# Eight smaller output-weight products in tiles 7 to 14 of the first head, a third query buffer, and last-head loads one a tile

## The chip, the cores and the metric

The kernel runs on one core of a Trainium2 chip. A core has five engines that run side by side and wait for each other by semaphores: TensorE (PE in the profile) multiplies, VectorE (DVE), ScalarE (ACT) and GpSimd (POOL) work on elements, and SyncE (SP) here only starts transfers. TensorE writes to PSUM, the others read PSUM (GpSimd does not) and SBUF. 16 DMA engines carry all transfers. The metric is the device time of one execution in microseconds (us); lower is better.

## The reference, cut to what matters

The input `x` has 2048 rows of 256. Two residual blocks follow, each normalised on the way in and on the way out:

- Attention, 16 heads of 128. The weights are 4-bit codes with a scale for every 32 input rows. `w = codes * scale`; q, k, v are `ln(x) @ w + b`; `attn = softmax(q k^T / sqrt(128))`; the heads' outputs are multiplied by the output weights `wo` (2048 by 256), and `bo` is added. `x = x + ln(that)`.
- A mixture of eight experts with top-2 routing, `silu(g) * u` between products of width 176, all experts computed and combined with the routing weights. `x = x + ln(that)`.

## The kernel before

**Tiles.** A step `g` of the main loop is one tile: 128 query rows `t` (0 to 15) of one head `h` (0 to 15), so 256 tiles and two steps to run empty. In each step TensorE makes the scores of 128 rows by 2048 keys in two halves (`scores_half`, L511, L512, L515: q and k are held as a high and a low 16-bit part, three products each). VectorE takes the row maximum of each half from PSUM (L516). ScalarE makes `p = exp(s - m)` with the row sums (`softmax`, L527). One step later ScalarE writes the normalised high part `ph` (L541), and VectorE the remainder `pl` in two halves (`low_half`, L556: p times the reciprocal sum, minus ph). SP transposes ph and pl by DMA (L544, L562) into `pth` and `ptl`. TensorE multiplies those with v, six matmuls to a piece, two pieces a step, 13 pieces behind the scores (`pv_part`, L582); every four tiles the result is evicted and written to DRAM (`ot_d`, L597 to L602).

**Work between.** `fill` gives each step one projection: q or k of the coming tiles and head (`proj_qk`) or v (`proj_v`). In the first six tiles of the first head two blocks of 128 rows of v are projected per step; ScalarE makes the high part and VectorE the low one (L269, L270), and the PSUM tile is free only then. Later projections go through `t32`, filled by ScalarE (L246, L277), from which GpSimd makes both parts (L247, L248, L278, L279). `weight_steps` loads and multiplies the q, k, v weights of the next pair of heads on GpSimd (L132, L138, L182, L184).

**Output weights.** They are loaded at the start, four pairs of codes and scales (`wo_raw`, L314 to L324), and multiplied on GpSimd by `dequant_wo` (L637 to L642), one pair in each of tiles 0 to 3 of the first head (L876).

**Buffers.** Most working tiles share one ring of 21 buffers of 4 KB a partition (`tag="x"`, `NX`): ph, pl, k, v, wo and its raw tiles, raw expert weights, reloaded attention outputs (`oi`), rows of x and others. A tile takes a buffer that has become free; if none is, the engine that writes it waits for the last reader of the one it takes. q has its own two buffers (L217); the last head puts two of its q tiles into the ring (`slot="x"`).

**Order.** Each engine runs its instructions in the order in which this program issues them. SP's order holds the transposes and, between them, the loads of the last heads: `early` (head 14, L793) loads `bo` and the first `oi`, `late` (head 15, L810) follows the tables `GW_LOAD` and `GW_SPLIT` (gate weights, loaded and split into two parts), `OI_LOAD` and `OI_USE` (attention outputs reloaded and multiplied by wo, `op_mm`, L712).

**Drain.** After the loop (L1107 on) the last pieces of v are multiplied, with output products `op_mm`, layer norms, transposes and the router between them; then the experts.

Of the kernel before, what the change touches and what calls it, by code (L numbers as in the profile page):

```python
# [8 lines left out]
F32 = mybir.dt.float32  # L9
F32R = mybir.dt.float32r  # L10
BF = mybir.dt.bfloat16
HP = mybir.dt.float16
# [3 lines left out]
ALU = mybir.AluOpType  # L16
# [5 lines left out]
D = 256  # L22
# [11 lines left out]
NX = 21  # L34
# [3 lines left out]
def sandwich(  # L38
# [22 lines left out]
    nc = tc.nc  # L61
# [45 lines left out]
    small = ctx.enter_context(tc.tile_pool(name="small", bufs=4))  # L107
# [85 lines left out]
    kqv = ctx.enter_context(tc.tile_pool(name="kqv", bufs=2))  # L193
# [20 lines left out]

    def kq_tile(which, h, b):
        if which == "q":
            return kqv.tile([128, 2, 512], HP, name="qT", bufs=2)  # L217
        if b % 2 == 0:
            KP[h] = kqv.tile([128, 2, 2, 512], HP, name="kT", tag="x", bufs=NX)
        return KP[h][:, b % 2]  # L220

    def proj_qk(which, h, b, tag="pj", wide=None, slot=None):
        w = W[(h // 2, which)]
        bias = bqs[:, IX[which], h : h + 1]
        ps = proj_psum(tag)
        col = bass.ts(h % 2, 128)
        n = 0
        for kc in range(2):
            for hl in range(2):
                nc.tensor.matmul(  # L230
                    ps, w[:, kc, col], xnT[:, 4 * b : 4 * b + 4, hl * 2 + kc, :],
                    start=(n == 0), stop=(n == 3),
                )
                n += 1
        if slot is None:
            t = kq_tile(which, h, b)
        else:
            t = kqv.tile([128, 2, 512], HP, name="qT_l", tag="x", bufs=NX)
        if wide is None:
            nc.scalar.activation(t[:, 0, :], ps, AF.Identity, bias=bias)  # L240
            pending.append(lambda: nc.vector.scalar_tensor_tensor(
                t[:, 1, :], ps, bias, t[:, 0, :], ALU.add, ALU.subtract
            ))
        else:
            t32 = wide.tile([128, 512], F32, name="t32")
            nc.scalar.activation(t32, ps, AF.Identity, bias=bias)  # L246
            nc.gpsimd.tensor_copy(t[:, 0, :], t32)  # L247
            nc.gpsimd.tensor_tensor(t[:, 1, :], t32, t[:, 0, :], ALU.subtract)  # L248
        (Q if which == "q" else K)[(h, b)] = t
# [31 lines left out]
    wo = []  # L281
    wo_raw = {}
# [3 lines left out]
    with tc.tile_pool(name="start", bufs=4) as st:  # L286
# [18 lines left out]
        for i, (which, codes, scales) in enumerate(  # L305
# [3 lines left out]
            cd = st.tile([128, 2, 256], F32, name="cd0", bufs=3)  # L309
# [4 lines left out]
        for q in range(4):  # L314
            hs = slice(4 * q, 4 * q + 4)
# [72 lines left out]
        mvs, rs, nbs, xns, xps = {}, {}, {}, {}, {}  # L388
# [111 lines left out]
    soft = soft_ctx.enter_context(tc.tile_pool(name="soft", bufs=2, reuse_waits="tile"))  # L500
# [73 lines left out]
    def pv_part(h, b, e):  # L574
# [11 lines left out]
        if e == 7:  # L586
# [20 lines left out]
    QK = {0: ("q", 0, 1), 2: ("k", 1, 0), 4: ("q", 0, 2), 6: ("k", 1, 1),  # L607
          8: ("q", 0, 3), 10: ("k", 1, 2), 12: ("q", 1, 0), 14: ("k", 1, 3)}

    def fill(h, t):  # L610
        p = h // 2
        if h == 0 and t < 6:
            proj_v(0, 4 + 2 * t, 2, "pv")
        if h == NH - 1:
            if t < 3:
                proj_qk("q", h, t + 1, wide=soft, slot="x" if t > 0 else None)
        elif t in QK:
            kind, dh, b = QK[t]
            if h + dh < NH:
                proj_qk(kind, h + dh, b, wide=soft)  # L620
        elif h % 2 == 0:
            if t in (3, 5) and h > 0:
                proj_v(p, 12 + (t - 3) // 2, 1, wide=soft)
            elif t == 7 and h > 0:
                proj_v(p, 14, 2, wide=soft)
            elif t >= 9 and p + 1 < NH // 2:
                proj_v(p + 1, (t - 9) // 2, 1, wide=soft)
        elif p + 1 < NH // 2:
            proj_v(p + 1, 4 + t // 2, 1, wide=soft)
# [4 lines left out]
            pv_part(n // 4, n % 4, e)  # L634


    def dequant_wo(q):  # L637
        sc, cd = wo_raw.pop(q)
        if q % 2 == 0:
            wo.append(kqv.tile([128, 8, D], BF, name="wo", tag="x", bufs=NX))  # L640
        hs = slice(4 * (q % 2), 4 * (q % 2) + 4)
        nc.gpsimd.tensor_tensor(wo[q // 2][:, hs], cd, sc, ALU.mult)  # L642

    def bias_row():
        pb = psA.tile([128, 512], F32, name="pb", tag="pj")
# [21 lines left out]
    def load_gu(src, i, pool, tag, bufs, eng=None):  # L667
        kc, eh = divmod(i, 2)
        stg = pool.tile([128, 4, I], F32, name="gu_raw", tag=tag, bufs=bufs)
        (eng or nc.sync).dma_start(  # L670
            out=stg,
            in_=src.rearrange("e (kc p) i -> kc p e i", p=128)[kc][:, 4 * eh : 4 * eh + 4],
        )
        return stg
# [25 lines left out]
    gw, crow, brow = None, None, None  # L700
    gst = {}
# [75 lines left out]
    def ln_c(b):  # L777
# [1 line left out]

    X1 = {}  # L780
    XV = x.rearrange("b (c p t) d -> p (b c) t d", p=128, t=4)
    GW_LOAD = {0: 1, 3: 2, 5: 3}
    GW_SPLIT = {4: 0, 6: 1, 8: 2, 10: 3}
    OI_LOAD = {
        2: (0, 1, 0), 4: (0, 1, 1), 6: (0, 1, 2), 9: (1, 0, 0), 10: (1, 0, 1),
        12: (0, 0, 3), 13: (0, 1, 3), 14: (1, 0, 2),
    }
    OI_USE = {
        4: (0, (0,)), 5: (0, (1,)), 6: (0, (2,)), 8: (1, (0,)), 9: (1, (1,)), 10: (1, (2,)),
        14: (0, (3,)), 15: (1, (3,)),  # L790
    }

    def early(t):  # L793
        nonlocal crow, brow
        if t == 7:
            cb = kqv.tile([128, 2, D], F32, name="crow", tag="x", bufs=NX)
            crow, brow = cb[:, 0], cb[:, 1]
            nc.sync.dma_start(out=brow, in_=bo.partition_broadcast(128))
        if t == 9:
            gst["b3"] = bias_row()  # L800
        if t == 11:
            bias_row2(gst.pop("b3"))
        if t == 13:
            nc.gpsimd.tensor_tensor(crow, crow, brow, ALU.add)
        if t in (8, 10, 12):
            load_oi(0, 0, t // 2 - 4)
        if t == 14:
            gst[0] = load_gu(wg, 0, kqv, "x", NX)

    def late(t):  # L810
        nonlocal gw
        if t == 3:
            proj_ctx.close()
            rp = ctx.enter_context(tc.tile_pool(name="gw", bufs=1, side="right"))
            gw = rp.tile([128, 2, 2, NCH, 128], F32R)
        if t in OI_USE:
            op_mm(0, *OI_USE[t], "pj", 2)
        if t in GW_SPLIT:
            split_gu(gw, GW_SPLIT[t], gst.pop(GW_SPLIT[t]), True)
        if t in GW_LOAD:  # L820
            i = GW_LOAD[t]
            gst[i] = load_gu(wg, i, kqv, "x", NX)
        if t in OI_LOAD:
            load_oi(*OI_LOAD[t])
        if t == 8:
            X1[0] = kqv.tile([128, 4, D], F32, name="x1_0", tag="x", bufs=NX)
            nc.sync.dma_start(out=X1[0], in_=XV[:, 0])

# [3 lines left out]
    for g in range(NS + 2):  # L832
        h, t = divmod(g, NT)
        live = g < NS
        if live:
            m = small.tile([128, 8], F32, name="m", bufs=6)
            s0 = scores_half(h, t, 0, m)
            if g == 0:
                proj_v(0, 0, 2)
                proj_v(0, 2, 2, "pv")  # L840
        if prev is not None:
            recip(prev[2])
        if prev2 is not None:
            low_half(1, *prev2)
        flush()
        if defer:
            pv_unit(2 * g - 1)
            defer = False
        pv_unit(2 * g)
        if prev is not None:  # L850
            prev = (*prev, high_part(*prev))
        if live:
            s1 = scores_half(h, t, 1, m)
            negmax(m)
            p = softmax((s0, s1), m)
        if prev is not None:
            low_half(0, *prev)
        prev2 = prev
        first = live and (2 * g + 1 - PVLAG) % 8 == 0
        if not first:  # L860
            pv_unit(2 * g + 1)
        if live:
            fill(h, t)
        if first and h == NH - 1:
            defer = True
        elif first:
            pv_unit(2 * g + 1)
        if live:
            prev = (h, t, m, p)
        else:  # L870
            prev = None
        if live:
            weight_steps(h, t)
        if h == 0 and t in (8, 9):
            tail_consts(t - 8)
        if g < 4:  # L876
            dequant_wo(g)
        if h == NH - 2:
            early(t)
        if h == NH - 1:  # L880
            late(t)
        if g == NS:
            ln_a(0)
        if g == NS + 1:
            load_oi(1, 0, 3)
            ust = [load_gu(wu, 0, kqv, "x", NX)]
            ust += [load_gu(wu, i, kqv, "x", NX) for i in range(1, 4)]
            ln_b1(0)
# [222 lines left out]
    uw = uwp.tile([128, 2, 2, NCH, 128], F32R)  # L1111
    d0 = load_d(0)
    d1 = load_d(4)
    op_mm(1, 0, (0, 1), "s")
    ln_b2(0)
    split_gu(uw, 0, ust[0], True)
    ln_c(0)
# [2 lines left out]
    tr(0, 0, "s")  # L1120
    tr(0, 1, "s")
    split_gu(uw, 1, ust[1], False)
    op_mm(1, 0, (2, 3), "s")
    for j in range(4):
        load_oi(1, 1, j)
    router_a(0, "s")
# [50 lines left out]
    for q in range(4 * NCH + 2):  # L1177
        b, c = divmod(q, NCH)
# [60 lines left out]
```

## Time and profile before

| what | us |
|---|---|
| median of three runs | 1842.27 (1839.41 to 1844.51) |
| profiled execution, and its span | 1839.29, 1837.5 |
| TensorE busy | 1780.7 (97%) |
| VectorE busy | 1635.1 (89%) |
| ScalarE busy | 1371.9 (75%) |
| GpSimd busy | 943.3 (51%) |
| L642, the four products for wo | 9.4 (2.36 each), from 41.6 to 60.7 us |
| L556, pl, 512 instructions | 730.3 (1.426 each; 1.265 at least, 4.340 at most) |

A line of a group names the source line, the engine, the operation and `output<-inputs`, with the count, busy time and mean. A line in order of time begins with start and duration; in brackets stands the idle time before it and what ended it. In busy time by stretch each engine has its busy us and instructions, then the granted TensorE clock (1.00 is full), the mean busy share of the DMA engines and their rate. A wait is `who <- for whom: us in all, times, longest`. SPq is SP's queue of transfers.

### The profile page before, as it was taken

What the parts mean: (1) busy time and instruction counts of PE and PEld (TensorE: products, weight loads), DVE (VectorE), ACT (ScalarE), POOL (GpSimd) and SP (SyncE); (2) the same over time, 40 slices, a digit from 0 to 9 for tenths busy, and PEclk for the clock granted to TensorE, in tenths of its full rate; (3) what the DMA queues carried; (4) which work ended last, traced back from release to release, by engine and by line L of the source; (5) the groups of instructions that cost most, each with busy time, mean ns of one, the idle gap of its engine ahead of it and who ended that gap; (6) DMA issues with size and microseconds to landing.
All of it is one profiled execution on the core that took longest, in us unless ns stands there. A gap on an engine that the chain in (4) does not pass through costs nothing. (4 is left out here: it accounts for less than half of the span.)

```text
span 1837.5 us, 25510 instructions
## 1 busy us (share of the span) xinstructions
PE 1780.7 (97%) x8890; PEld 936.4 (51%) x8890; DVE 1635.1 (89%) x2269; ACT 1371.9 (75%) x1732; POOL 943.3 (51%) x911
## 2 busy tenths in 40 slices
PE   7699999999999999999999999999999999899997
PEld 4344444444444444444444444444444444588886
DVE  7899999999999999999999999999999978558665
ACT  5688888888888888888888888888888877322232
POOL 3456556565656565656565656566444332323232
PEclk9899999999999999999999999999999999999999
DMA  7799999999999999999999999999999999921000
GB/s 172 136 196 203 199 199 199 203 202 189 200 207 193 201 198 208 194 200 198 199 199 198 204 205 202 194 205 198 191 190 194 216 217 227 310 83 35 1 13 23
DMA packets 1092336, 330.70 MB, mean 180 GB/s; under 512 B 1069728, under 2 KB 1079280, under 8 KB 1092208
## 3 DMA queue, kind: packets, MB, share of 16 engines
q1 hardware_dynamic: 1081744, 301.02, 89.8%
q0 software_dynamic: 9920, 27.82, 5.7%
q8 instruction: 70, 1.15, 0.2%
q14 instruction: 58, 0.48, 0.1%
q10 hardware_dynamic: 544, 0.23, 0.0%
HBM read 41.68 MB, written 18.87 MB: 33 GB/s over the span
## 5 line engine op out<-in xcount | busy, mean ns | idle before, releaser
L527 ACT ACTIVATE p<-s,m,ssc 128x1024 f32<-128x1024 f32 x512 | 612.2, 1200 | 182.7 <-DVE m L520 176.0
L556 DVE SCALAR_TENSOR_TENSOR pl<-p,m,ph 128x1024 f16<-128x1024 f32 x512 | 730.3, 1426 | 9.1 <-ACT ph L541 7.0
L516 DVE TENSOR_REDUCE m<-s 128x1 f32<-128x1024 f32 x512 | 622.0, 1215 | 37.1 <-PE s L515 34.9
L541 ACT ACTIVATE ph<-p,m 128x2048 f16<-128x2048 f32 x256 | 512.8, 2003 | 62.3 <-ACT t L246 17.3
L582 PE MATMUL pv<-pth,v 128*128 128x512 f16 x2048 | 506.3, 380 | 10.5 <-issue 5.1
L582 PEld LDWEIGHTS <-v 128*128 128x128 f16 x3072 | 301.0, 98 | 378.1 <-issue 10.0
L511 PE MATMUL s<-kT,qT 128*128 128x512 f16 x992 | 377.3, 380 | 5.9 <-ACT p L527 5.2
L512 PE MATMUL s<-kT,qT 128*128 128x512 f16 x992 | 377.2, 380 | 0.0
L515 PE MATMUL s<-kT,qT 128*128 128x512 f16 x992 | 296.0, 380 | 0.0
L582 PE MATMUL pv<-ptl,v 128*128 128x512 f16 x1024 | 253.1, 380 | 0.0
L247 POOL CAST qT<-t 128x512 f16<-128x512 f32 x61 | 76.4, 1252 | 231.7 <-ACT t L246 231.7
L278 POOL CAST v<-t 128x256 f16<-128x256 f32 (+1 forms) x105 | 44.0, 419 | 256.8 <-ACT t L277 256.8
L279 POOL TENSOR_TENSOR v<-t,v 128x256 f16<-128x256 f32 (+1 forms) x105 | 163.0, 1552 | 8.5
L515 PEld LDWEIGHTS <-qT 128*128 128x128 f16 x992 | 97.3, 98 | 118.0 <-issue 1.6
L512 PEld LDWEIGHTS <-qT 128*128 128x128 f16 x992 | 97.3, 98 | 114.0 <-issue 11.6
L511 PEld LDWEIGHTS <-qT 128*128 128x128 f16 x992 | 97.3, 98 | 106.3 <-issue 2.2
L1004 POOL TENSOR_TENSOR hh<-sg,hh 128x512 fp32r<-128x512 f32 x42 | 55.1, 1311 | 143.4 <-ACT hh L1003 108.4
L1003 ACT CAST hh<-sg 128x512 fp32r<-128x512 f32 (+1 forms) x45 | 27.5, 611 | 107.1 <-DVE sg L1015 107.0
L527 ACT ACTIVATION_READ_ACCUMULATOR p<-s,m,ssc 128x1 f32 x512 | 99.0, 193 | 0.0
L599 POOL TENSOR_TENSOR o<-t,o 128x512 f16<-128x512 f32 x63 | 93.6, 1486 | 5.2
L247 POOL CAST kT<-t 128x512 f16<-128x512 f32 x60 | 64.8, 1080 | 60.3 <-ACT t L246 56.5
L258 PE MATMUL pj<-wv,xnT 128*128 128x256 bf16 x512 | 75.9, 277 | 16.2 <-DVE v L270 16.1
(197 smaller groups left out, 1894.7 us busy)
## 6 DMA issues: line engine op xcount, KB each, us to landing
oi<-ot_d SPq DMA_DIRECT2D x32, 512.0 KB, 5.5
ot_d<-o POOLq DMA_DIRECT2D x63, 256.0 KB, 4.5
pth<-ph SPq DMA_TRANSPOSE x256, 5.1
ptl<-pl SPq DMA_TRANSPOSE x256, 5.4
xt<-in_L_attn_x SPq DMA_DIRECT2D x4, 512.0 KB, 4.2
woc<-in_L_attn_wo_codes SPq DMA_DIRECT2D x4, 512.0 KB, 8.7
wos<-in_L_attn_wo_scales SPq DMA_DIRECT2D x16, 128.0 KB, 8.1
x<-in_L_attn_x SPq DMA_DIRECT2D x4, 512.0 KB, 5.0
```

Source lines behind the costliest of these rows:

```text
L247: nc.gpsimd.tensor_copy(t[:, 0, :], t32)
L258: nc.tensor.matmul(ps[:, bass.ts(j, 256)], xnT[:, t0 + j, hl * 2 + kc, :], w[:, kc, :], start=(i == 0), stop=(i == 3),)
L279: nc.gpsimd.tensor_tensor(v[:, 1, sl, :], t32, v[:, 0, sl, :], ALU.subtract)
L511: nc.tensor.matmul(s[:, j, :], q[:, 0, qc], k[:, 0, :], start=True, stop=False)
L512: nc.tensor.matmul(s[:, j, :], q[:, 0, qc], k[:, 1, :], start=False, stop=False)
L515: nc.tensor.matmul(s[:, j, :], q[:, 1, qc], k[:, 0, :], start=False, stop=True)
L516: nc.vector.tensor_reduce(m[:, half : half + 1], s, AX.XY, ALU.max)
L527: nc.scalar.activation(p[:, bass.ts(i, 1024)], s, AF.Exp, bias=m[:, 2:3], scale=ssc[:, 0:1], accum_out=m[:, 3 + i : 4 + i],)
L541: nc.scalar.activation(ph, p, AF.Copy, scale=m[:, 6:7])
L556: nc.vector.scalar_tensor_tensor(pl[:, cs], p[:, cs], m[:, 6:7], ph[:, cs], ALU.mult, ALU.subtract)
L582: nc.tensor.matmul(ps, V[(h // 2, c // 4)][:, i % 2, c % 4, dc], d[:, :, c, :], start=(n == 0), stop=(n == 47),)
L599: nc.gpsimd.tensor_tensor(o[:, :, 1, :], halves(t32), o[:, :, 0, :], ALU.subtract)
```

## The change

`dequant_wo` now multiplies half of what it did (two heads' rows, 512 elements a partition) and is called in tiles 7 to 14 of the first head. `qT` has three buffers, and the last head's three q tiles, projected in tiles 0, 1 and 4, all use them. `crow` moves to a small tile of its own, and `brow` takes a ring buffer alone. Of the loads in the last head, the first gate load moves from tile 14 of head 14 to tile 2, and the others shift so that a tile has one load at most; splits, products and the closing of the projection pools shift with them. In the drain the third group of products of block 1's first half moves ahead to the first two.

```diff
--- before.py
+++ after.py
@@ -214,12 +214,12 @@
 
     def kq_tile(which, h, b):
         if which == "q":
-            return kqv.tile([128, 2, 512], HP, name="qT", bufs=2)
+            return kqv.tile([128, 2, 512], HP, name="qT", bufs=3)
         if b % 2 == 0:
             KP[h] = kqv.tile([128, 2, 2, 512], HP, name="kT", tag="x", bufs=NX)
         return KP[h][:, b % 2]
 
-    def proj_qk(which, h, b, tag="pj", wide=None, slot=None):
+    def proj_qk(which, h, b, tag="pj", wide=None):
         w = W[(h // 2, which)]
         bias = bqs[:, IX[which], h : h + 1]
         ps = proj_psum(tag)
@@ -232,10 +232,7 @@
                     start=(n == 0), stop=(n == 3),
                 )
                 n += 1
-        if slot is None:
-            t = kq_tile(which, h, b)
-        else:
-            t = kqv.tile([128, 2, 512], HP, name="qT_l", tag="x", bufs=NX)
+        t = kq_tile(which, h, b)
         if wide is None:
             nc.scalar.activation(t[:, 0, :], ps, AF.Identity, bias=bias)
             pending.append(lambda: nc.vector.scalar_tensor_tensor(
@@ -607,13 +604,15 @@
     QK = {0: ("q", 0, 1), 2: ("k", 1, 0), 4: ("q", 0, 2), 6: ("k", 1, 1),
           8: ("q", 0, 3), 10: ("k", 1, 2), 12: ("q", 1, 0), 14: ("k", 1, 3)}
 
+    LASTQ = {0: 1, 1: 2, 4: 3}
+
     def fill(h, t):
         p = h // 2
         if h == 0 and t < 6:
             proj_v(0, 4 + 2 * t, 2, "pv")
         if h == NH - 1:
-            if t < 3:
-                proj_qk("q", h, t + 1, wide=soft, slot="x" if t > 0 else None)
+            if t in LASTQ:
+                proj_qk("q", h, LASTQ[t], wide=soft)
         elif t in QK:
             kind, dh, b = QK[t]
             if h + dh < NH:
@@ -634,12 +633,13 @@
             pv_part(n // 4, n % 4, e)
 
 
-    def dequant_wo(q):
-        sc, cd = wo_raw.pop(q)
-        if q % 2 == 0:
+    def dequant_wo(j):
+        sc, cd = wo_raw[j // 2]
+        if j % 4 == 0:
             wo.append(kqv.tile([128, 8, D], BF, name="wo", tag="x", bufs=NX))
-        hs = slice(4 * (q % 2), 4 * (q % 2) + 4)
-        nc.gpsimd.tensor_tensor(wo[q // 2][:, hs], cd, sc, ALU.mult)
+        hs = slice(2 * (j % 4), 2 * (j % 4) + 2)
+        rs = slice(2 * (j % 2), 2 * (j % 2) + 2)
+        nc.gpsimd.tensor_tensor(wo[j // 4][:, hs], cd[:, rs], sc[:, rs], ALU.mult)
 
     def bias_row():
         pb = psA.tile([128, 512], F32, name="pb", tag="pj")
@@ -779,22 +779,22 @@
 
     X1 = {}
     XV = x.rearrange("b (c p t) d -> p (b c) t d", p=128, t=4)
-    GW_LOAD = {0: 1, 3: 2, 5: 3}
-    GW_SPLIT = {4: 0, 6: 1, 8: 2, 10: 3}
+    GW_LOAD = {2: 0, 4: 1, 6: 2, 8: 3}
+    GW_SPLIT = {5: 0, 7: 1, 9: 2, 11: 3}
     OI_LOAD = {
-        2: (0, 1, 0), 4: (0, 1, 1), 6: (0, 1, 2), 9: (1, 0, 0), 10: (1, 0, 1),
+        3: (0, 1, 0), 5: (0, 1, 1), 7: (0, 1, 2), 9: (1, 0, 0), 10: (1, 0, 1),
         12: (0, 0, 3), 13: (0, 1, 3), 14: (1, 0, 2),
     }
     OI_USE = {
-        4: (0, (0,)), 5: (0, (1,)), 6: (0, (2,)), 8: (1, (0,)), 9: (1, (1,)), 10: (1, (2,)),
+        5: (0, (0,)), 6: (0, (1,)), 7: (0, (2,)), 8: (1, (0,)), 9: (1, (1,)), 10: (1, (2,)),
         14: (0, (3,)), 15: (1, (3,)),
     }
 
     def early(t):
         nonlocal crow, brow
         if t == 7:
-            cb = kqv.tile([128, 2, D], F32, name="crow", tag="x", bufs=NX)
-            crow, brow = cb[:, 0], cb[:, 1]
+            crow = small.tile([128, D], F32, name="crow", bufs=1)
+            brow = kqv.tile([128, D], F32, name="brow", tag="x", bufs=NX)
             nc.sync.dma_start(out=brow, in_=bo.partition_broadcast(128))
         if t == 9:
             gst["b3"] = bias_row()
@@ -804,12 +804,10 @@
             nc.gpsimd.tensor_tensor(crow, crow, brow, ALU.add)
         if t in (8, 10, 12):
             load_oi(0, 0, t // 2 - 4)
-        if t == 14:
-            gst[0] = load_gu(wg, 0, kqv, "x", NX)
 
     def late(t):
         nonlocal gw
-        if t == 3:
+        if t == 5:
             proj_ctx.close()
             rp = ctx.enter_context(tc.tile_pool(name="gw", bufs=1, side="right"))
             gw = rp.tile([128, 2, 2, NCH, 128], F32R)
@@ -822,7 +820,7 @@
             gst[i] = load_gu(wg, i, kqv, "x", NX)
         if t in OI_LOAD:
             load_oi(*OI_LOAD[t])
-        if t == 8:
+        if t == 11:
             X1[0] = kqv.tile([128, 4, D], F32, name="x1_0", tag="x", bufs=NX)
             nc.sync.dma_start(out=X1[0], in_=XV[:, 0])
 
@@ -873,8 +871,8 @@
             weight_steps(h, t)
         if h == 0 and t in (8, 9):
             tail_consts(t - 8)
-        if g < 4:
-            dequant_wo(g)
+        if 7 <= g < 15:
+            dequant_wo(g - 7)
         if h == NH - 2:
             early(t)
         if h == NH - 1:
@@ -1111,7 +1109,7 @@
     uw = uwp.tile([128, 2, 2, NCH, 128], F32R)
     d0 = load_d(0)
     d1 = load_d(4)
-    op_mm(1, 0, (0, 1), "s")
+    op_mm(1, 0, (0, 1, 2), "s")
     ln_b2(0)
     split_gu(uw, 0, ust[0], True)
     ln_c(0)
@@ -1120,7 +1118,7 @@
     tr(0, 0, "s")
     tr(0, 1, "s")
     split_gu(uw, 1, ust[1], False)
-    op_mm(1, 0, (2, 3), "s")
+    op_mm(1, 0, (3,), "s")
     for j in range(4):
         load_oi(1, 1, j)
     router_a(0, "s")
```

## Prediction

> **What bounds the kernel now.** I read the times, then the page's busy shares, then busy time by stretch, then the engines' instructions in order of time where a stretch is not full, the waits of the last head, and the chain of waits. TensorE is busy 97% of the span, so the question is where the other 3% is and whether the change touches it.
>
> ```profile
> core 0: us, PE busy (x) PEld busy (x) DVE busy (x) ACT busy (x) POOL busy (x), PEclk, DMA share, GB/s
> 28.00:85.00 57.00, 38.57 (x181) 18.68 (x180) 48.63 (x57) 34.95 (x45) 20.91 (x18) 0.88 0.60 110
> 85.00:145.00 60.00, 59.97 (x286) 27.88 (x285) 57.81 (x72) 50.56 (x64) 35.71 (x46) 1.00 1.09 192
> 205.00:1400.00 1195.00, 1190.77 (x5706) 557.58 (x5705) 1139.08 (x1426) 1018.49 (x1268) 702.20 (x684) 1.00 1.11 199
> 1465.00:1510.00 45.00, 40.95 (x203) 20.23 (x201) 32.84 (x44) 32.62 (x40) 17.04 (x13) 0.92 1.10 218
> ```
>
> From 85 us to 1400 us TensorE is full (1190.77 of 1195): nothing shortens that but less matmul work, and the change removes none. VectorE has only 3.6% left there (57.81 of 60). What is open is 28 to 85 us, the first seven tiles, and the last head with the drain, from 1465 us. In the first, VectorE in order of time, GpSimd beside it, shows why:
>
> ```profile
> 41.70 3.38 DVE L556 SCALAR_TENSOR_TENSOR pl<-p,m,ph 128x1024 f16<-128x1024 f32 x1 [0.17 <-ACT ph L541]
> 46.44 2.71 DVE L556 SCALAR_TENSOR_TENSOR pl<-p,m,ph 128x1024 f16<-128x1024 f32 x1
> 59.86 4.34 DVE L556 SCALAR_TENSOR_TENSOR pl<-p,m,ph 128x1024 f16<-128x1024 f32 x1
> ...
> 41.64 2.35 POOL L642 TENSOR_TENSOR wo<-woc,wos 128x1024 bf16<-128x1024 f32 x1
> 45.70 2.36 POOL L642 TENSOR_TENSOR wo<-woc,wos 128x1024 bf16<-128x1024 f32 x1
> 58.43 4.67 POOL L642 TENSOR_TENSOR wo<-woc,wos 128x1024 bf16<-128x1024 f32 x2
> ```
>
> L556 takes 1.27 us undisturbed. These three end 1.09 us after the L642 beside them (43.99, 48.06 and 63.10, against ends at 45.08, 49.15 and 64.20): VectorE stands still until GpSimd is done. That is 2.11 + 1.44 + 3.07 = 6.6 us, in tiles where VectorE sets the pace. The late subtraction of v (L270) then holds the PSUM tile of the next projection, and TensorE comes back cold:
>
> ```profile
> 49.80 1.89 PE L258 MATMUL pj<-wv,xnT 128*128 128x256 bf16 x8 [5.38 <-DVE v L270]
> 67.49 1.89 PE L258 MATMUL pj<-wv,xnT 128*128 128x256 bf16 x8 [4.74 <-DVE v L270]
> 76.16 1.05 PE L258 MATMUL pj<-wv,xnT 128*128 128x256 bf16 x8 [2.67 <-DVE v L270]
> ```
>
> 1.89 us against 1.05 is half clock. In the last head the waits, and then the end of the loop in order of time (ScalarE, SP's queue, TensorE), show two more places:
>
> ```profile
> ACT ph L541 <- DMA ptl<-pl: 7.5, 1, 7.5
> PE s L511 <- ACT p L527: 4.0, 1, 4.0
> ```
>
> ```profile
> 1562.52 2.00 ACT L541 ACTIVATE ph<-p,m 128x2048 f16<-128x2048 f32 x1 [1.07 <-DVE m L537]
> ...
> 1569.34 2.66 SPq L544 DMA_TRANSPOSE pth<-ph  x1
> ...
> 1575.44 7.22 PE L582 MATMUL pv<-pth,v 128*128 128x512 f16 x24 [5.14 <-issue]
> ```
>
> A write of ph waits 7.5 us for the transpose that frees its buffer. At the end ph is ready at 1564.5, but SP starts its transpose 4.8 us later: SP runs without a gap from 1500.0 to 1575.9. The queue of transposes sets the end there, and TensorE stands 5.14 us for it.
>
> **The change, part by part.**
>
> *L642 leaves tiles 0 to 3.* Run forward with the row durations: VectorE's work of one such tile is 6.03 us (64.12 to 70.15, undisturbed). After the v subtraction TensorE needs 0.9 (v projection) + 0.87 (q or k, even tiles) + 1.3 (half a score tile) = 2.2 or 3.1 us until VectorE's next reduction, in which VectorE has 2.8 us of other work; so tiles take 6.0 to 6.6 us by turns. First reductions now at 37.95, 45.00, 54.85, 64.12, 72.23, 79.49 and 85.67; without L642 I get 37.95, 43.0, 49.6, 55.8, 62.4, 68.6 and 74.8: 10.9 us earlier at tile 7. TensorE's gaps become about 2.2 us. The rows are ambiguous on whether that still cools it: after 2.37 us (58.47) there was none, after 2.67 us matmuls go from 0.38 to 0.63 us a moment later. The Trainium skill (TensorE: Matmul & The Clock Gate, "HAM oscillation") asks for idle windows of about 3.4 us before the clock drops; by that none would, and the gain is the whole 10.9. By the 2.67 row it can. I allow one cold stretch, priced by 49.80 to 54.65: 4.85 us for 3.06 of work, 1.8. **-9.1 us**, bounds -5 and -11; the lower is the 6.6 less one cold stretch.
>
> *Eight pieces in tiles 7 to 14.* 512 elements cost 1.27 us (L184, same shape and types), so 8 x 1.27 = 10.2 us of GpSimd, against 9.4 before. GpSimd has room (35.71 of 60). In its queue each piece stands behind the q, k or v conversion, weight loads and L99 to L105 of its tile, and ahead of the next conversion. Those have tiles to spare, but they hold the two t32 buffers, which ScalarE fills: a backlog over some 6 us would stop it. The price is VectorE's. The skill (SBUF — State Buffer, "Who interferes with whom") says that a VectorE operation with two SBUF inputs and a GpSimd one exclude each other for a whole instruction, whoever starts first; it speaks against this part: all eight in the way make up to 10.2 us, less VectorE's slack of some 1.6 (2.19 in 60, for 45 us): +8.6. The row: L556 averages 1.426 against 1.265 over 512, 82 us in all, 76 without L642, over about 320 two-input GpSimd operations of the loop (L279 105, L599 63, L248 123, L184 24): 0.24 each, 1.9 for eight, as a GpSimd operation that meets a running L556 waits itself and then fits under the reductions. Tile 13 is worse: its piece follows L184 directly, as the two L642 at 58.43 did, one more 1.2. 3.1 less 1.6 of slack: **+1.5 us**, bounds 0 and +8.6, nearer the row.
>
> *Buffers held longer.* The eight raw tiles of the output weights stay in the 21 shared buffers until tiles 8 to 14. Held in tile 7: 8 raw, 2 + 1 of k, 4 of v, 1 wo = 16, leaving 5 for ph and pl. A ph lives from 98.7 to about 107.3, a pl from 101.1 to about 112, with a period of 5.7: four at once at most. **0**, by one buffer; without it, rival 4.
>
> *Third query buffer, crow apart, loads one a tile.* Held at tile 3 of the last head: before k 2, v 4, wo 2, crow 1, oi 4, gu_raw 3, qT_l 2 = 18, three left, which is the 7.5 us wait. After, at most 15. TensorE's stall (4.05 idle, then 5.2 for 2.6 at half clock: 6.65) goes. But SP issues the same transposes and loads from 1421 on; the first load of Wg, moved from tile 14 of head 14 to tile 2 of the last, crosses eight transposes, the other Wg loads six or eight, those of oi two, x1 six, all in the stretch where SP is behind. Tiles with a load take about 6.75 us on SP, those without 5.8, whoever waits; so TensorE reaches the end earlier and waits longer. Kept: SP's one gap, 1498.6 to 1500.0. **-1.4 us**; bounds -6.65, if SP's durations are mostly waits, and +3, if three loads in a row (tiles 12 to 14) now wait behind a deeper lag. The q conversion moved from tile 2 to 4 (1.46 + 1.16 on GpSimd) is read in tile 12: free. The eviction L743 is now one tile ahead of the next product into its PSUM tile, not two; it took 3.1 us from the product's end, TensorE's other work 5.2. If that cover went, at most 3 us.
>
> *Drain.* 16 matmuls, 1.75 us (L727), move into the 5.14 us gap. Behind it the chain of waits is TensorE from 1575.44 to 1604.4, so they come off it: at 1585.28 the router products find xT ready (L907 ends at 1585.04). **-1.75 us**, bounds 0 and -3.8 (with the cold restart at 1575.44, 2.0, gone).
>
> Sum: -9.1 + 1.5 + 0 - 1.4 - 1.75 = -10.75 us, on the profiled execution's 1839.29 us (span 1837.5 and 1.8 around it): 1828.5. That is 0.16% under the median, so on 1842.27 the same share, 0.58%, gives **1831.5 us**.
>
> **Rivals.** (1) The pieces hit VectorE nearly every time: +8.6 for +1.5, -3.7 us, 1838.6. For it: 3.6% slack, and GpSimd 79% busy in 103 to 115. Against: 0.24 us each. (2) TensorE stays cold in most early tiles: -5 for -9.1, -6.7, 1835.6. For it the 2.67 row, against it the 2.37 row. (3) The last head keeps its 6.65: -16, 1826.2. For it, a stall really goes; against it, SP without a gap. (4) Slower: five free buffers are too few in tiles 7, 8 and 10, as a transpose can land 8.2 us after issue against a median of 5. Priced by the one stall seen, 3 x 6.65 = +20: net +9.2, 1851.5. It decides from two such stalls on (13.3 against 10.75). Against it: four are needed.
>
> **How the numbers follow.** Forecast 0.60, its own range 1826 to 1836; rival 1 0.13, rival 2 0.10, rival 3 0.07, rival 4 0.10. Three in a thousand, 5.5 us, is about what a measurement tells from no change. Forecast and rival 3 are beyond it (0.67), rival 2 in 0.07 of its 0.10, rival 1 in 0.03 of its 0.13: faster 0.77. Within: 0.03 + 0.08 = 0.11. Slower: 0.10 + 0.02 = 0.12. From 1824 to 1841 only rival 4 and the ends of the bounds are left out.
>
> **What would show it.** No L556 over 2.5 us before tile 7, first reductions 5.8 to 6.8 us apart there, TensorE full from about 74 us. L556 in tiles 7 to 14 up by some 0.2 us in the mean. No ph wait over 2 us in the last head, but SP still without gaps and the last transpose as late after ph. Three groups of products ahead of the last pv. Wrong: ph waiting on a transpose in tiles 6 to 10; TensorE idle over 3 us in tiles 8 to 15.

## The result, and the profile after

The changed kernel takes **1828.96 us** (median of four runs, 1827.29 to 1830.16) against 1841.74 us for the kernel before beside it (four runs, 1839.41 to 1844.51): a ratio of 0.9929, 95% interval 0.9912 to 0.9947. Faster, as forecast; 1831.5 us was predicted. The profiled execution took 1827.29 us, its span is 1825.4.

I cut both profiled spans at fixed points: the first row maximum of a tile (L516 before, L513 after), the start of the last 24 v products, and the first gate product.

| stretch | before, us | after, us | difference | predicted |
|---|---|---|---|---|
| start to tile 1 | 37.95 | 37.55 | -0.4 | 0 |
| tiles 1 to 7 | 47.72 | 39.03 | -8.7 | -9.1 |
| tiles 7 to 16 | 53.02 | 53.17 | +0.15 | +1.5 |
| tiles 16 to 24 | 46.50 | 46.73 | +0.2 | 0 |
| tiles 24 to 240 | 1268.80 | 1269.83 | +1.0 | 0 |
| tile 240 to the last v products | 121.45 | 119.93 | -1.5 | -1.4 |
| those to the first gate product | 25.96 | 23.50 | -2.5 | -1.75 |
| the rest | 236.10 | 235.66 | -0.4 | 0 |
| span | 1837.5 | 1825.4 | -12.1 | -10.75 |

Busy time by stretch of the changed kernel, with the columns of the first profile above:

```profile
core 0: us, PE busy (x) PEld busy (x) DVE busy (x) ACT busy (x) POOL busy (x), PEclk, DMA share, GB/s
28.00:85.00 57.00, 44.10 (x221) 21.45 (x220) 49.88 (x68) 42.38 (x54) 17.28 (x19) 0.97 0.74 137
75.00:85.00 10.00, 10.00 (x48) 4.48 (x46) 9.54 (x14) 8.57 (x11) 4.99 (x5) 1.00 0.95 166
85.00:145.00 60.00, 58.91 (x283) 27.51 (x282) 57.52 (x72) 50.92 (x64) 48.04 (x54) 1.00 1.09 197
205.00:1400.00 1195.00, 1190.22 (x5704) 557.37 (x5702) 1138.58 (x1427) 1017.77 (x1268) 698.13 (x682) 1.00 1.10 199
1465.00:1510.00 45.00, 45.00 (x250) 24.27 (x249) 37.69 (x48) 36.83 (x41) 13.80 (x10) 1.00 1.11 229
```

TensorE does 221 instead of 181 matmuls between 28 and 85 us and is full from 75 us on; the middle is as it was. From 1465 to 1510 us it is full too (40.95 of 45 before). In the first tiles, VectorE and then TensorE in order of time:

```profile
41.30 1.28 DVE L553 SCALAR_TENSOR_TENSOR pl<-p,m,ph 128x1024 f16<-128x1024 f32 x1 [0.17 <-ACT ph L538]
44.06 1.27 DVE L553 SCALAR_TENSOR_TENSOR pl<-p,m,ph 128x1024 f16<-128x1024 f32 x1
47.28 1.28 DVE L553 SCALAR_TENSOR_TENSOR pl<-p,m,ph 128x1024 f16<-128x1024 f32 x1
```

```profile
45.98 1.05 PE L255 MATMUL pj<-wv,xnT 128*128 128x256 bf16 x8 [1.97 <-DVE v L267]
52.61 1.05 PE L255 MATMUL pj<-wv,xnT 128*128 128x256 bf16 x8 [2.13 <-DVE v L267]
58.86 1.52 PE L255 MATMUL pj<-wv,xnT 128*128 128x256 bf16 x8 [1.97 <-DVE v L267]
67.54 1.05 PE L255 MATMUL pj<-wv,xnT 128*128 128x256 bf16 x8 [2.49 <-DVE v L267]
```

pl takes its undisturbed 1.27 us. The waits for v fell from 5.38 and 4.74 to 1.97 to 2.49 us, and one projection still runs slow (1.52 for 1.05). The end of the loop, on TensorE:

```profile
1541.74 3.59 PE L727 MATMUL op<-wo,oi 128*128 128x256 bf16 x16 [7.31 <-DMA oi<-ot_d]
1561.00 5.40 PE L727 MATMUL op_s<-wo,oi 128*128 128x256 bf16 x48
1566.24 5.34 PE L579 MATMUL pv<-pth,v 128*128 128x512 f16 x24
1572.29 1.91 PE L727 MATMUL op_s<-wo,oi 128*128 128x256 bf16 x16
1575.21 1.55 PE L915 MATMUL rp_s<-xT,rw 128*8 128x512 f32 x6 [1.01 <-DVE xT L905]
```

The 5.14 us gap ahead of the last v products is gone, and they run at full clock (5.34 for 7.22). But TensorE now stands 7.31 us for an attention output in tile 14, and 1.01 us for xT: the stalls moved.

### The profile page after: what moved, and what is told of

The parts are those of the page before. It is cut to its first block, busy times and chain, and to the rows that moved or that the text cites. A ratio compares the mean times of both kernels' runs of the same rounds, so it can differ in the third digit from the quotient of the medians.

```text
span 1825.4 us, 25498 instructions
## 1 busy us (share of the span) xinstructions
PE 1774.1 (97%) x8890; PEld 934.3 (51%) x8890; DVE 1630.7 (89%) x2269; ACT 1371.8 (75%) x1732; POOL 948.0 (52%) x915
## 5 line engine op out<-in xcount | busy, mean ns | idle before, releaser
L553 DVE SCALAR_TENSOR_TENSOR pl<-p,m,ph 128x1024 f16<-128x1024 f32 x512 | 725.7, 1417 | 1.3 <-ACT ph L538 1.3
L513 DVE TENSOR_REDUCE m<-s 128x1 f32<-128x1024 f32 x512 | 622.4, 1216 | 35.7 <-PE s L512 33.5
L508 PE MATMUL s<-kT,qT 128*128 128x512 f16 x1024 | 388.8, 380 | 3.1 <-ACT p L524 2.5
L509 PE MATMUL s<-kT,qT 128*128 128x512 f16 x1024 | 388.8, 380 | 0.7 <-POOL kT L245 0.7
L512 PE MATMUL s<-kT,qT 128*128 128x512 f16 x1024 | 304.9, 379 | 0.0
L512 PEld LDWEIGHTS <-qT 128*128 128x128 f16 x1024 | 100.3, 98 | 122.0 <-issue 1.5
L509 PEld LDWEIGHTS <-qT 128*128 128x128 f16 x1024 | 100.3, 98 | 114.5 <-issue 8.5
L508 PEld LDWEIGHTS <-qT 128*128 128x128 f16 x1024 | 100.4, 98 | 109.3 <-issue 1.4
L245 POOL TENSOR_TENSOR kT<-t,kT 128x512 f16<-128x512 f32 x60 | 88.9, 1481 | 5.1
```

The source lines that it names most:

```text
L508: nc.tensor.matmul(s[:, j, :], q[:, 0, qc], k[:, 0, :], start=True, stop=False)
L509: nc.tensor.matmul(s[:, j, :], q[:, 0, qc], k[:, 1, :], start=False, stop=False)
L512: nc.tensor.matmul(s[:, j, :], q[:, 1, qc], k[:, 0, :], start=False, stop=True)
L513: nc.vector.tensor_reduce(m[:, half : half + 1], s, AX.XY, ALU.max)
L553: nc.vector.scalar_tensor_tensor(pl[:, cs], p[:, cs], m[:, 6:7], ph[:, cs], ALU.mult, ALU.subtract)
```

## The experiments

The shortened diffs of the first five are against the kernel before, the others against the changed one. Times are medians; the kernel before is the one run beside each.

**Only the output weights: eight pieces in tiles 7 to 14.** The diff shows the call; the halved slices are those of the whole change.

```diff
...
-        if g < 4:
-            dequant_wo(g)
+        if 7 <= g < 15:
+            dequant_wo(g - 7)
```

> Only the output-weight products move to eight pieces in tiles 7 to 14. Theory (the four products lock VectorE out in tiles 0 to 3, and TensorE is full from tile 7 on): first reductions of tiles 1 to 7 as in the changed kernel, tile 7 some 8.7 us earlier, then 1.4 us given back by tile 16; -7.3 us in all, about 1834.4. Rival (the gain of the early tiles needs the other parts, or is given back where the pieces run): within 2 us of the kernel before, 1840 to 1843.

1829.98 us (six runs, 1826.13 to 1836.16), ratio 0.9926 [0.9911, 0.9942]. Tiles 1 to 7 take 39.02 us, 7 to 16 53.13: the stretches of the whole change, so this part owns them. The time expected, 1834.4, was missed: it gained 13.4 us, where its stretches up to tile 24 show 8.4. A part is that the profiled run of before, 1839.3, lies 4.1 us under the median beside this kernel (1843.4, 22 runs); the rest is open.

**Fills in place of the products**, in the old tiles; the product with the scales is left out, so the output weights are a constant.

```diff
-        nc.gpsimd.tensor_tensor(wo[q // 2][:, hs], cd, sc, ALU.mult)
+        for _ in range(3):
+            nc.gpsimd.memset(wo[q // 2][:, hs], 0.01)
```

> In tiles 0 to 3 each of the four products is replaced by three fills of the same output with a constant: GpSimd writes, but reads nothing; the product of codes and scales is left out. Theory (VectorE's two-input operation and a GpSimd operation that reads SBUF exclude each other): no L556 over 2 us beside the fills, and tile 7 some 8 to 9 us earlier with nothing given back, about 1833. Rival (GpSimd's time or its queue in these tiles is what counts, whatever it does): L556 and tile 7 as before, about 1841.7.

1831.41 us (1829.85 to 1833.51), ratio 0.994 [0.9925, 0.9955]; tiles 1 to 7 in 38.17 us. GpSimd and VectorE of this kernel in order of time:

```profile
41.22 2.97 POOL L643 MEMSET wo<- 128x1024 bf16 x3
45.87 2.99 POOL L643 MEMSET wo<- 128x1024 bf16 x3
```

```profile
41.29 1.28 DVE L556 SCALAR_TENSOR_TENSOR pl<-p,m,ph 128x1024 f16<-128x1024 f32 x1 [0.17 <-ACT ph L541]
47.28 1.27 DVE L556 SCALAR_TENSOR_TENSOR pl<-p,m,ph 128x1024 f16<-128x1024 f32 x1
```

GpSimd is as busy beside L556 as before (2.97 against 2.35 us), yet L556 takes 1.28 us, not 3.38. The stall came from GpSimd reading SBUF beside VectorE's operation with two SBUF inputs, not from GpSimd being busy, or from its place in the order. GpSimd doesn't need two inputs for it: in the kernel before, the casts of L598 take 0.61 us (median) with no L556 beside them, and 1.54 us if they start during one.

**Four whole products, but late**, in tiles 7, 9, 11 and 13.

```diff
-        if g < 4:
-            dequant_wo(g)
+        if 7 <= g < 15 and g % 2 == 1:
+            dequant_wo((g - 7) // 2)
```

> Four whole products of 2.36 us in tiles 7, 9, 11 and 13 of the first head, everything else as before. Theory (a piece of 1.27 us fits under VectorE's reductions of 1.5 us between two L556, a whole one doesn't): L556 beside them up to 3 us, tiles 7 to 16 about 3 us longer than with eight pieces (53.1 us there, 56 here); total about 10 us under the kernel before, 1833. Rival (only the move matters, the full stretch absorbs either size): tiles 7 to 16 within 0.5 us of 53.1 us and the time of the kernel with only the pieces moved.

1834.75 us (1833.95 to 1836.56), ratio 0.996 [0.9947, 0.9973]. Tiles 7 to 16 take 56.55 us, 3.5 more than before the change; the pieces cost 0.15 there. GpSimd and VectorE:

```profile
99.84 2.36 POOL L642 TENSOR_TENSOR wo<-woc,wos 128x1024 bf16<-128x1024 f32 x1
110.47 2.37 POOL L642 TENSOR_TENSOR wo<-woc,wos 128x1024 bf16<-128x1024 f32 x1
```

```profile
100.49 2.79 DVE L556 SCALAR_TENSOR_TENSOR pl<-p,m,ph 128x1024 f16<-128x1024 f32 x1
110.30 3.63 DVE L556 SCALAR_TENSOR_TENSOR pl<-p,m,ph 128x1024 f16<-128x1024 f32 x1
```

Both L556 end 1.08 to 1.09 us after the product beside them; the second is recorded as starting 0.17 us ahead of it and is held all the same, so the recorded start alone doesn't say who goes first. So the move alone leaves a part of the price, and halving the products takes it away.

**Only the last head's part** (third query buffer, `crow` apart, loads one a tile).

```diff
-            return kqv.tile([128, 2, 512], HP, name="qT", bufs=2)
+            return kqv.tile([128, 2, 512], HP, name="qT", bufs=3)
...
-    GW_LOAD = {0: 1, 3: 2, 5: 3}
+    GW_LOAD = {2: 0, 4: 1, 6: 2, 8: 3}
```

> Only the third query buffer, crow apart and the shifted loads of the last head; products for wo and the drain as before. Theory (SP's queue of transposes and loads sets the end of the loop): the 7.5 us wait of ph and TensorE's 4 us stall at tile 3 are gone, but the first pv of the last group starts only about 1.5 us earlier; 1840.2. Rival (the stall itself is what the last head loses): 6.65 us earlier, about 1835.1.

1837.38 us (nine runs, 1834.97 to 1842.5), ratio 0.9972 [0.996, 0.9985]. From tile 240 to the last v products 119.51 us, 1.9 less than before, not 6.65. With the old drain those products wait 0.35 us and run at full clock; from there to the first gate product it is 1.5 us shorter.

```profile
1575.25 5.34 PE L579 MATMUL pv<-pth,v 128*128 128x512 f16 x24 [0.35 <-issue]
```

In time it gained 2.8 to 7.4 us by the interval, which doesn't rule out the rival's 6.65; its two stretches show 3.4. The rival is set aside by the stretches, not by the time.

**Only the drain's order.**

```diff
-    op_mm(1, 0, (0, 1), "s")
+    op_mm(1, 0, (0, 1, 2), "s")
...
-    op_mm(1, 0, (2, 3), "s")
+    op_mm(1, 0, (3,), "s")
```

> Only the third group of products of block 1 moves ahead of the last pv. Theory: it fills 1.75 us of TensorE's 5.14 us gap and comes off the chain behind it; a gap of 3.4 us is left, so the pv behind it still run cold (7.2 us for 24): -1.75 us, about 1840.0. Rival (with the gap shorter the clock stays up): -3.8 us, about 1837.9. Second rival (the transposes of block 0 are waited for anyway): 0.

1841.01 us (14 runs, 1837.23 to 1848.25), ratio 0.9998 [0.9986, 1.001]: nothing measurable. In the profile, TensorE:

```profile
1566.68 5.40 PE L727 MATMUL op_s<-wo,oi 128*128 128x256 bf16 x48
1575.50 6.81 PE L582 MATMUL pv<-pth,v 128*128 128x512 f16 x23 [3.41 <-issue]
```

The gap shrank from 5.14 to 3.41 us and the drain by 1.96, but the v products stay cold: this order alone doesn't give the 5.34 us.

By their ratios the three parts gain 0.74, 0.28 and 0.02%, 1.04% in all, where the whole change gains 0.71%, each to some 0.15; by the stretches they gain 8.4, 3.4 and 2.0 us, 13.8 in all, against 12.1 of the span. So the shares of the parts are read from the stretches. In time the pieces alone (1829.98 us) can't be told from the whole change (1828.96): that the other two parts add something beside them, the stretches alone show.

**Last-head loads issued by GpSimd.**

```diff
-            load_oi(*OI_LOAD[t])
+            load_oi(*OI_LOAD[t], eng=nc.gpsimd)
```

and the same for the gate loads and the rows of x: 13 loads leave SP's queue.

> The changed kernel, with the 13 loads of the last head issued from GpSimd's queue. Theory one (SP's issuing of transposes and loads in order is what is late): the last pv group starts up to 5 us earlier, as SP has some 12 us less to issue; about 17 us under the kernel before. Theory two (the DMA engines themselves are full there): the last transpose lands within 1.5 us of where it does in the changed kernel, about 12.5 us under the kernel before.

1827.19 us (1824.67 to 1833.97), ratio 0.9923 [0.9908, 0.9938]. TensorE of this kernel:

```profile
1547.05 5.00 PE L579 MATMUL pv<-pth,v 128*128 128x512 f16 x12 [8.70 <-DMA pth<-ph]
1571.52 6.81 PE L579 MATMUL pv<-pth,v 128*128 128x512 f16 x23 [3.41 <-DMA pth<-ph]
```

With fewer transfers in SP's queue the transposes still arrive late, and the last v products start 124.34 us after tile 240 (119.93 in the changed kernel). Neither theory's mark was met: not 5 us earlier, and not within 1.5 us, but 4.4 later. On GpSimd's queue three loads are issued close together (1527.15, 1527.72 and 1529.87), and a transpose of pl beside them stays 12.15 us in SP's queue:

```profile
1529.14 12.15 SPq L559 DMA_TRANSPOSE ptl<-pl  x1
```

So loads issued elsewhere delay the transposes too, which speaks for the DMA engines that all transfers share and against the place in SP's queue. It is not shown cleanly, as the edit also moved the loads closer together.

**Gate loads in tiles 0 to 3 of head 14**, none in the last head.

```diff
-    GW_LOAD = {2: 0, 4: 1, 6: 2, 8: 3}
+    GW_LOAD = {}
...
+        if t < 4:
+            gst[t] = load_gu(wg, t, kqv, "x", NX)
```

> The changed kernel, with the four loads of Wg in tiles 0 to 3 of head 14, where SP's queue still has gaps, and not in the last head. Theory (SP's queue sets the end of the loop, 0.9 us for a load): the last group of pv starts 3.6 us earlier than in the changed kernel, counted from tile 240; about 16 us under the kernel before, 3.5 under the changed one. Rival (the four buffers held for a head make ph wait, or the queue is not what sets the end): no earlier, or later, than the changed kernel.

1826.79 us (1822.24 to 1828.96), ratio 0.991 [0.9895, 0.9924]. The last v products start 115.84 us after tile 240, 4.1 sooner than in the changed kernel; tiles 224 to 240 take 98.64 us for 96.14, so 1.6 us stay. TensorE's wait for oi in tile 14 falls from 7.31 to 3.8 us. As the loads leave SP's queue and the DMA engines alike, this doesn't tell the two apart, and the time can't be told from the changed kernel's.

**19 buffers, and 20.**

```diff
-NX = 21
+NX = 19
```

> The changed kernel with 19 shared buffers for 21, so that 3 are left for ph and pl in tile 7 and not 5. Theory of the prediction (four are in use at once at most): ph or pl wait for a transpose in tiles 6 to 10, some 1 to 2 us each, TensorE loses 3 to 8 us there; 1832 to 1837. Rival (the margin is wider): tiles 7 to 16 take 53.1 us as in the changed kernel, and the time is its time.

> The changed kernel with 20 buffers in the shared pool in place of 21, so that four instead of five are free in tiles 7 to 14 of the first head. By the prediction's count (four at once are enough): tiles 7 to 16 in 53.0 to 53.4 us as with 21, time within 2 us of the changed kernel's. If the softmax needs five at once: tiles 7 to 16 in 54.5 to 56 us, as with 19 (55.9).

With 19: 1831.78 us (1830.72 to 1835.45), ratio 0.9949 [0.9935, 0.9964], tiles 7 to 16 in 55.91 us, 2.7 more than with 21 and a little under the 3 to 8 expected. ScalarE there:

```profile
84.44 2.00 ACT L538 ACTIVATE ph<-p,m 128x2048 f16<-128x2048 f32 x1 [2.26 <-DMA ptl<-pl]
102.36 2.00 ACT L538 ACTIVATE ph<-p,m 128x2048 f16<-128x2048 f32 x1 [1.74 <-DMA ptl<-pl]
```

With 20: 1828.39 us (1826.56 to 1831.5), ratio 0.9934 [0.992, 0.9947], tiles 7 to 16 in 54.34 us, 1.2 more. The time is the one that the count expected, the stretch fits neither expectation: a single write of ph comes late, at 108.10 after 2.53 us of idle ScalarE, where the count said that four are enough. The kernels differ in nothing else, so in this trace 21 have no buffer to spare, though the profile doesn't name what freed that one.

**Weight loads later**, to see whether the loads in tiles 0 to 5 of even heads make the transposes late (the last section shows that wait).

```diff
-            plan = {i: ("k", (i,)) for i in range(6)}
-            plan.update({8 + i: ("q", (i,)) for i in range(6)})
-            done = {7: "k", 15: "q"}
+            plan = {4 + i: ("k", (i,)) for i in range(6)}
+            plan.update({12 + i: ("q", (i,)) for i in range(4)})
+            done = {11: "k"}
...
```

> The changed kernel with the loads of the key weights moved from tiles 0 to 5 of the even heads to tiles 4 to 9 (their dequantisation from tile 7 to 11), the query weights' from tiles 8 to 13 to tiles 12 to 15 and 0 to 1 of the next head, and the value weights' one tile later. Theory one (the 2 to 5 us by which runs of one kernel differ between tiles 16 and 240 are TensorE waiting in tile 7 of even heads for a transpose of p that the key loads made late): no wait of L579 for pth in tile 7 of heads 2 to 14, tiles 16 to 240 in 1315 to 1316.5 us (the best seen is 1315.3, the changed kernel's profiled run 1316.6, others up to 1322), time 1825 to 1827.5 with less spread than the changed kernel. Theory two (the transposes alone fill the DMA engines, and any load of the head makes some first product late): the wait moves to tile 11 or 15, tiles 16 to 240 stay between 1316 and 1322, time 1828 to 1831.

1826.81 us (1825.43 to 1828.11), ratio 0.9921 [0.9907, 0.9935]. Tiles 16 to 240 take 1316.76 us; two waits of 0.33 and 0.30 us are left, in tiles 18 and 58. Between the theories: the long waits are absent, but the kernel with 20 buffers, without this edit, has none in its profile either. Undecided.

**Both: gate loads in head 14, weight loads later.**

> The kernel with the Wg loads in tiles 0 to 3 of head 14, and with the weight loads of e9. If both gains stand beside each other: 1 to 2 us below the 1826.8 us of the earlier Wg loads alone (head 14 has no weight loads of its own, so the two don't meet): 1824 to 1826. If the weight loads change nothing: 1826 to 1828.

**1824.91 us** (1822.78 to 1826.61), ratio 0.9909 [0.9894, 0.9924]: the lowest median of all kernels here. Beside the last one (same tile 224 to 0.1 us) the last v products start 2.4 us sooner. Its interval still overlaps that of the changed kernel.

**No weight loads from the third pair of heads on.**

```diff
+        if p > 1:
+            raw[(p, which)] = last_raw[0]
+            return
...
```

> The changed kernel without the loads of the q, k and v weights of head pairs 2 to 7 (scales and codes stay those loaded last, so the heads from 4 on compute with other weights; all other work, the conversions on GpSimd among it, is as before). Theory one (these loads make the transposes of p late in some tiles, and that is what runs of one kernel differ by): no wait of L579 for pth from head 3 on, tiles 24 to 240 in 1268.5 to 1269.0 us (seen so far 1268.8 to 1275), all runs within 2.5 us of each other, time 1824.5 to 1827. Theory two (the transposes are late by themselves): waits of 0.3 to 2.6 us stay in some profile, runs differ by 4 us or more, and the median stays within 1.5 us of the changed kernel's 1829.

1840.23 us (11 runs, 1838.81 to 1840.56), ratio 0.9988 [0.9979, 0.9997]: fewer transfers, and 11 us **slower** than the changed kernel. No wait for pth is left and the runs agree to 1.75 us (those of before beside it: 1839.07 to 1846.99), as theory one said; the time is as neither said. The group of pl in the changed kernel and in this one says where it went:

```profile
L553 DVE SCALAR_TENSOR_TENSOR pl<-p,m,ph 128x1024 f16<-128x1024 f32 x512 | 725.7, 1417 | 1.3 <-ACT ph L538 1.3
```

```profile
L559 DVE SCALAR_TENSOR_TENSOR pl<-p,m,ph 128x1024 f16<-128x1024 f32 x512 | 744.3, 1454 | 1.3 <-ACT ph L544 1.3
```

18.6 us more in pl. One place, tile 40 to 41, in the changed kernel (GpSimd, VectorE), then in this one:

```profile
278.16 2.04 POOL L245 TENSOR_TENSOR qT<-t,qT 128x512 f16<-128x512 f32 x1
277.92 1.26 DVE L553 SCALAR_TENSOR_TENSOR pl<-p,m,ph 128x1024 f16<-128x1024 f32 x1
```

```profile
278.02 1.16 POOL L251 TENSOR_TENSOR qT<-t,qT 128x512 f16<-128x512 f32 x1
278.47 1.78 DVE L559 SCALAR_TENSOR_TENSOR pl<-p,m,ph 128x1024 f16<-128x1024 f32 x1
```

In the first VectorE started first and GpSimd waited; in the second GpSimd was first, and pl ends 1.07 us after it. Without the load instructions GpSimd reaches its conversions at other moments, and VectorE waits more often: 67 of the pl operations take more than 1.6 us, 43 in the changed kernel. Tiles that are longer for this reason also give the transposes more time, so the run doesn't settle what makes them late.

## Why the prediction was right, and where not

**L642 out of tiles 0 to 3** (-9.1, measured -8.7). The mechanism stands: the fills show that it is the product's reading of SBUF. The forward run to tile 7 took 36.85 us from tile 1. Of the eleven profiles without products in tiles 0 to 3, three took 36.98 or 36.99 us, at a full clock (the kernel with 20 buffers and the two with later weight loads); four took 38.1 to 38.2 and four 39.0, the changed kernel's among them, each with one slow stretch. That the allowance for one stretch came true was therefore luck. What the prediction weighed for it, the length of the wait, does not decide it alone: waits of 1.97 to 2.13 us were followed by 1.52 us at 58.86 in the changed kernel and by 1.05 in the one with 20 buffers. The rule weighed against the row there (The Trainium skill, TensorE: Matmul & The Clock Gate, "HAM oscillation": windows of some 3.4 us) would have allowed no slow stretch; the trace has one after waits of at most 2.13 us, so it is no safe bound here.

The clock records of the 14 traces say more. All 38 slow stretches between 20 and 1800 us last 3.41 us or two or three times that, and in each trace their edges lie on one grid of 3.41 us, which falls on another place of the program each time. In the interval of the grid ahead of a slow stretch TensorE was busy 42% of the time or less; no interval at full clock with less than 42% was followed by full clock. The changed kernel, two intervals, and the one with 20 buffers:

```profile
core 0: us, PE busy (x), PEclk, DMA share, GB/s
55.87:59.28 3.41, 1.44 (x9) 1.00 0.88 169
59.28:62.69 3.41, 3.41 (x12) 0.50 1.06 238
55.45:58.86 3.41, 1.77 (x8) 1.00 1.07 179
```

1.44 of 3.41 us is 42%, 1.77 is 52%. So in these traces it counts how much idle time falls into one interval, and with gaps of 2 us that depends on where the grid lies. This was worked out after the runs and none tested it; the three profiles at full clock also come from one chip, so a difference between chips is not excluded.

**The pieces** (+1.5, measured +0.15 in tiles 7 to 16 and +0.2 to tile 24): the mis-sized term. The prediction took 0.24 us a piece and 1.2 for tile 13. The sixteen L553 of tiles 7 to 14 add up to 24.0 us, the same sixteen before to 23.45: 0.55 in all, 0.07 a piece. Single ones pay: beside the piece at 111.91 and the q conversion that it moved, L553 takes 2.24 us at 112.59 for 1.27 before; beside the piece at 115.81, 1.96 for 1.43. Others gain, as a piece pushes the next operation out of the way: L553 at 100.93 takes 1.61 us for 2.15. And tile 13 costs nothing new:

```profile
122.08 1.27 POOL L184 TENSOR_TENSOR wk<-st_c,st_s 128x512 bf16<-128x512 f32 x1
123.30 2.26 POOL L642 TENSOR_TENSOR wo<-woc,wos 128x512 bf16<-128x512 f32 x1
```

```profile
122.15 2.27 DVE L553 SCALAR_TENSOR_TENSOR pl<-p,m,ph 128x1024 f16<-128x1024 f32 x1
```

L553 waits for L184, as it did before (2.28 us at 130.83), and then goes first: the piece (2.26 for 1.27) waits for it. The two GpSimd operations don't hold VectorE as a pair, which the two whole products at 58.43 did. The size counts too: whole products in the same tiles cost 3.5 us. An average over 320 operations of other tiles was the wrong row; when each operation starts is what decides. (The slack of 3.6%, said there of 85 to 1400 us, is that of 85 to 145; the row from 205 to 1400 leaves 4.7%.)

**Buffers** (0, "by one buffer"): right at 21, but the working was not. With 20 four are free, which the count called enough, and a write of ph waited; in that trace five were needed, so rival 4 was one buffer away, not two. With 19 its price was 2.7 us in all, not 6.65 a stall.

**Last head** (-1.4, measured -1.5, alone -1.9). The 7.5 us wait for ph and TensorE's 6.65 went, and TensorE lost the time again, but not where the prediction put it. It had TensorE wait longer for the last transposes, and the last one as late behind ph as before. In the changed kernel the last transpose of ph starts 1.8 us after ph is ready (4.8 before), and the last v products don't wait. TensorE stands in tile 14, at 1541.74, waiting for oi (7.31 us, 1.75 before) and cold (3.59 for 1.92). Its load is the first of the three in a row (tiles 12 to 14) for which the prediction had only the bound of +3. So the number agrees and the place does not, which is in part luck. Rival 3 fell. Whether SP's queue or the DMA engines behind it set the end stays open: taking 13 loads off that queue brought nothing, but moved them closer together; taking transfers out of the head (4.1 us) relieves both.

**Drain** (-1.75, measured -2.5). The moved products gave their 1.75. The cold restart, left at 2.0 as a bound, went as well: -1.9. And "the router products find xT ready" failed: xT waits on ScalarE behind a conversion of the up weights (L661), which waits for its load; +1.0. Neither part alone does both: the order alone leaves 3.41 us of gap and a cold restart, the last head's part alone leaves 0.35 and a warm one.

**The scale.** The medians differ by 12.8 us and the profiled spans by 12.1, where the sum said 10.75 and its scaled form 10.8. Most of what the sum lacked lies in its terms, the pieces (1.35) and the drain (0.75) above all. The profiled run of before was quick, 1839.3 us against medians of 1841.3 to 1843.4 in later comparisons, but so was that of the changed kernel, the fastest of its four.

**The signs.** As forecast, no L553 before tile 7 takes over 2.5 us, and TensorE is full from 75 us. First reductions were to be 5.8 to 6.8 us apart there; they are 4.95, 6.73, 5.88, 8.67 (the slow stretch), 6.25 and 6.55. L553 in tiles 7 to 14 was to take 0.2 us more in the mean; it takes 0.03 more. A write of ph in the last head waits 9.72 us, at 1549.42: behind TensorE's stall in tile 14, not for a transpose, as the reciprocal that it needs ends only at 1549.34.

## What to carry to other kernels

Move a GpSimd operation that reads SBUF away from tiles in which VectorE sets the pace, and cut it to a size that fits between VectorE's two-input operations; judge it by the times of both engines, not by a mean. When a stall in a stretch full of transfers is removed, look for it again later in that stretch, as in the last head here. Before trusting a difference of a few us, look at how far the profiled run stands from the median.

## What the runs showed of the hardware that was not expected

**Some transposes land late.** TensorE of the kernel with only the pieces, whose profiled run was its slowest (1836.16 us):

```profile
451.09 1.47 PE L582 MATMUL pv<-pth,v 128*128 128x512 f16 x6 [2.04 <-DMA pth<-ph]
641.11 1.47 PE L582 MATMUL pv<-pth,v 128*128 128x512 f16 x6 [2.58 <-DMA pth<-ph]
```

These are the first v products of a group, at the end of step 6 of heads 4 and 6, ahead of the scores of tile 7. They need the transposes of tiles 0 to 3, the last of which lands just in time or not; profiles of other kernels have none to three such waits, 0.15 to 2.6 us each, and tiles 16 to 240 take from 1315.3 to 1322.0 us (the kernel without weight loads, 1333.1, apart): 1315.3 to 1317.1 in the profiles without such waits, 1320.9 and 1322.0 in those with most of it (4.99 and 2.95 us). What makes them late stayed open, and as each kernel has one profile, so did whether runs of one kernel differ by it.

**Less work can slow VectorE.** Without 108 instructions on GpSimd (915 to 807), the same 512 pl operations took 18.6 us more: the rest started at other moments, and VectorE was held more often.
